# A four-layer graph network on one core: the second filter product is issued before the nodes' turn, and turns are inserted, removed and moved

## The chip, the core and the metric

The kernel runs on one NeuronCore of a Trainium2 chip. The number that counts is the device time of one execution, in microseconds. The kernel before takes 1591.17 us (median of three runs, 1591.0 to 1591.64). A profiled execution of it, from which all finer numbers here are read, took 1607.39 us, of which 1605.5 us lie between its first and its last instruction.

The engines are called as in the profile: PE (matrix products), PEld (its weight loads), DVE (vector work), ACT (activation functions), POOL (GpSimd), SP (issues DMAs).

## What is computed

128 graphs of 64 nodes, 128 features each, go through four layers. Every layer is `x = layernorm(x + f(x, adj))`. Cut to what matters:

```python
# layers 0 and 1: a continuous filter over the edges (i, j) with adj != 0
W   = ssp(gauss(adj) @ w1 + b1) @ w2 + b2          # filter of an edge: two products
agg[i] = sum_j  (x @ w_in)[j] * W[i, j] * c(adj[i, j])
out = ssp(agg @ o1 + c1) @ o2 + c2                 # "the nodes' turn"
# layer 2: graph convolution, norm_A from adj
h = elu(elu(x @ W0 + b0));  h = elu(norm_A @ (h @ W1) + b1)
out = norm_A @ (h @ W2) + b2
# layer 3
out = relu((A_norm @ x) @ W.T + b)
```

`ssp` is `softplus - log 2`. The entries of `adj` at 5.0 or more weigh nothing in layer 0, and zero entries carry one constant filter.

## The kernel before, in words

The function at work is `sparse_stack`. It treats the graphs in 64 pairs (`NP`), two graphs on the 128 partitions. The nodes of each graph are sorted so that the edges of a pair fill a compact list of slots. Preparing those lists (`gathering`, `compact`, `nearest`, `pack`) is vector work that is spread through the first half of the run as `early`, a few instructions per step.

**The main loop** is one Python loop over `i` that lays down the instruction streams, with `n, k = divmod(i, 3)`: `n` counts pairs (0 to 63 in layer 0, 64 to 127 in layer 1), and the slots of a pair are cut into three chunks `k`. A pass of the loop is called a step here. Each step works on three chunks at once, a pipeline of depth three: the current chunk `c`, the chunk before it `c1`, and the one before that, `c2`.

- `filter_in(c)`: first filter product (PE, tile `px`, line 1774), then the exponential (ACT).
- `gather(c1)`: product that fetches the features of the neighbours (PE, `pg`, line 1800), copied out by ACT.
- `softplus(c)`: the logarithm (ACT).
- `filter_out(c2)`: second filter product (PE, `pw`, line 1788).
- `message(c2)`: filter times features (DVE, `m`, line 1814). It empties `pw`.

`px`, `pg` and `pw` each have one PSUM buffer (`bufs=1`), of two banks. So the next `pw` may start only when `m` of the step before has read the last one, the next `px` only when the exponential has read the last, and the next `pg` only when its copy is done.

At `k == 0` a step also builds the weighted one-hot matrix for the gather (`hot`, DVE, line 1762), asks SP for the data of two pairs later, and starts preparing features for a later group (`ahead`). At `k < 2` ACT computes one half of the next pair's Gaussians (`d`). At the start of each step `run(sums, ...)` lays down some of the nine reductions of a pair's messages (`agg`, DVE, lines 1837 and 1841), and `run(early, ...)` some of the preparation.

**Turns.** The rest is written as Python generators, and a `yield` ends a turn. Each kind of work has a queue, and `slot(queue)` gives its first generator one turn. A turn that ends in `yield True` has just issued products into a bank of `ps_n` (two banks in all). The instruction that empties this bank is laid down not at once but inside the next call of `slot` for another queue, after that queue's own turn (the variable `owing`). The queues:

- `befores`: `node_before`, features for a group of four pairs: transposes `xT`, one turn; product `y`, one turn (lines 1444 and 1453). It also adds a bias on POOL (line 1449).
- `nodes`: `node_after`, once for each group of four pairs when its reductions are complete. In layer 0 first `zero_share` (transposes `zT`, product `zs`); then product `u` (line 1565), product `o` (1584), product `back` (1593), and a layer norm: two turns of statistics on DVE (lines 1415 and 1416), one turn on POOL (1422, 1423, and four of 1428, which write `x_all`).
- `convs[0]` and `convs[1]`: `graph_convs`, layers 2 and 3 for one group of four pairs, for even and odd groups. It starts when the group's layer 1 is done, and runs through the products `gx` (transposes), `gh`, `hw`, `nT` (transposes), `gh`, `hw`, `o`, a layer norm, `nT`, `sup`, `o`, and a layer norm. Its rows are stored by four scatters issued by POOL (`stores`, one per step).
- `last`: three queues for the last pairs (groups of two, one and one pairs), which run node work and convolutions in one chain.

A group of four pairs takes twelve steps. "Place 0" to "place 11" below mean the steps of a group, place 0 being `k = 0` of its first pair. In each step, PE's order before the change is `px`, `pg`, the nodes' turn, at `k == 1` the turn of `befores`, the turns of `last`, `pw`, then the turn of `convs[0]` and that of `convs[1]`. `in_order` pins the streams of all five engines to the order in which they are laid down, so no engine passes a waiting instruction.

After the loop, the tail gives one turn to each queue in rounds until all are empty:

```python
    run(sums, -1)
    while nodes or convs[0] or convs[1] or any(last.values()) or stores:
        for queue in (*last.values(), nodes, *convs):
            slot(queue)
        run(stores, 1)
```

Of the kernel before, what the change touches and what calls it, by code (L numbers as in the profile page):

```python
# [601 lines left out]
def sparse_stack(ctx: ExitStack, tc: tile.TileContext, t: dict, out: bass.AP, flag):  # L602
# [14 lines left out]
    NP = NB // 2  # L617
    GS = 4
# [12 lines left out]
    def pair_at(n):  # L631

        return n // NP, (n + 8 * (n // NP)) % NP
# [168 lines left out]
    def wait_steps(n):  # L802
        yield from (None for _ in range(n))
# [583 lines left out]
    def bank(name, n=GS):  # L1387
        ps = ps_n.tile([P, 512], F32, tag="n", name=name)[:, 0 : n * P]
        return ps, ps.rearrange("p (s c) -> p s c", s=n)
# [163 lines left out]
    def node_after(layer, q, agg):  # L1553


        w = layers[layer]
        name = f"{layer}_{q}"
        n = agg.shape[1]
        codes = node_codes.pop((layer, q))
        if layer == 0:  # L1560
            yield from zero_share(q, agg)
        elif q < len(GROUPS[1]) - 1:
            yield
        u, _ = bank(f"u_{name}", n)
        nc.tensor.matmul(
            u, lhsT=w["o1"], rhs=agg.rearrange("f s r -> f (s r)"), start=True, stop=True
        )
        yield True
        a, h = once("na", n, q), once("nh", n, q)
        act(h, u, AF.Identity, bias=w["c1"])  # L1570
        act(a, h, AF.Abs)
        act(a, a, AF.Exp, scale=-1.0)
        yield
        act(a, a, AF.Ln, scale=0.5, bias=half)

        back = once("bk", n, q)
        nc.vector.tensor_scalar(back, codes, row[:, 0:1], None, ALU.is_equal)
        back = by_pair(back)
        yield
        nc.vector.scalar_tensor_tensor(h, h, 0.0, a, ALU.max, ALU.add)  # L1580
        yield
        _, ps = bank(f"o_{name}", n)
        for s in range(n):
            nc.tensor.matmul(  # L1584
                ps[:, s, :], lhsT=h[:, s * P : (s + 1) * P], rhs=w["o2"], start=True, stop=True
            )
        yield True
        o = by_pair(once("no", n, q))
        act(o, ps, AF.Copy)
        yield  # L1590
        _, ps = bank(f"back_{name}", n)
        for s in range(n):
            nc.tensor.matmul(ps[:, s, :], lhsT=back[:, s, :], rhs=o[:, s, :], start=True, stop=True)
        yield True
        y = by_pair(once("ny", n, q))
        xs = x_all[:, GROUPS[layer][q], :]
        nc.vector.tensor_add(y, ps, xs)
        yield
        yield from layernorm(y, xs, n, name)
        if layer == 1:  # L1600
            if n < GS:
                yield from graph_convs(q)
            else:
                convs[q % 2].append(graph_convs(q))
# [58 lines left out]
    def graph_convs(q):  # L1663
# [3 lines left out]
        n = xs.shape[1]  # L1667
# [11 lines left out]

        if n == GS:  # L1680
            scaled(2, q)
            yield from wait_steps(2)
        flat, ps = bank(f"gx_{q}", n)
        for s in range(n):
            nc.tensor.transpose(ps[:, s, :], xs[:, s, :], ident)
# [36 lines left out]
        else:  # L1722
            nT3 = normals[3, q]
        y3 = yield from times("sup", lambda s: xs[:, s, :], lambda s: nT3[:, s, :])
        flat, ps = bank(f"o3_{q}", n)
        nc.tensor.matmul(
            flat, lhsT=ones, rhs=g["b3"][:, 0:n, :].rearrange("i s c -> i (s c)"),
# [147 lines left out]
    N = 2 * NP  # L1875
# [12 lines left out]

    def ahead(n):

        layer, p = pair_at(n + GS)
        for q, group in enumerate(GROUPS[layer]):
            if group.start == p:
                befores.append(node_before(layer, q))
# [21 lines left out]
    for i in range(3 * N + 2):  # L1916
# [1 line left out]
        c, c1, c2 = None, *past  # L1918


        run(sums, (1, 4, 4)[k])
        run(early, 9 if i < 18 else (PACE - 2, PACE + 1, PACE + 1)[k] if i < 3 * (NP - 8) else 7)
        run(side, min(2, len(side)))
        run(stores, 1)
# [13 lines left out]
        if n < N:  # L1938
            layer, p = pair_at(n)
            q = next(q for q, group in enumerate(GROUPS[layer]) if group.start <= p < group.stop)  # L1940
            c = dict(
                id=f"{n}_{k}", n=n, k=k, s=p - GROUPS[layer][q].start, at=(layer, q), w=layers[layer],
                size=CHUNKS[layer][p // 8],
            )
            if k == 0:
                if n + GS < N:
                    ahead(n)
                if n + 2 < N:
                    slot_data[n + 2], late = later_loads(n + 2)
                if c["s"] == min(2, len(range(NP)[GROUPS[layer][q]]) - 1):  # L1950
                    load_nodes(layer, q)
                if n > 0:
                    one_hot(n)
                if layer == 1 and c["s"] == 0 and q in last:
                    last[q].append(normals_of(q))
            if k == 1 and n + 2 < N:
                late()
            filter_in(c)
        if c1 is not None:
            gather(c1)  # L1960
        if c is not None:
            softplus(c)
            if k == 2 and sines:

                sines.popleft()()
        slot(nodes)
        if k == 1 and befores:
            slot(befores)
        for queue in last.values():
            slot(queue)  # L1970
        if c2 is not None:
            filter_out(c2)
            message(c2)
        if convs[0]:
            slot(convs[0])
# [59 lines left out]
```

## Time and profile before

| what | value |
|---|---|
| median of three runs | 1591.17 us |
| profiled execution / its span | 1607.39 us / 1605.5 us |
| PE busy | 1432.6 us, 89% |
| DVE busy | 1355.6 us, 84% |
| ACT busy | 1335.6 us, 83% |
| POOL busy | 732.5 us, 46% |
| main loop, first to last `px` | 75.3 to 1526.7 us |
| layer 0 in a group of twelve steps (`px` to `px`, 221 to 629 us) | 39.8 to 43.0 us |
| layer 1 in a group of twelve steps (878 to 1426 us) | 48.6 to 50.8 us |
| tail, from the last reductions of the loop | 1545.9 to 1605.5 us |

How to read it: busy time is summed over stages that differ. In layer 0 the preparation still runs and DVE is as busy as PE; in layer 1 the convolutions have joined and PE is the fullest; in the tail no engine is full. A wait counts only in the stage in which it lies. The time of a step is read from the starts of its `px`, and what ended an engine's idle time stands in brackets in the timeline.

### The profile page before, as it was taken

How to read it: one execution, taken by the hardware profiler on the slowest of the kernel's cores; microseconds unless marked ns; L12 is line 12 of the kernel's file. 1: busy time of each engine (PE TensorE's matmuls, PEld its weight loads, DVE VectorE, ACT ScalarE, POOL GpSimd, SP SyncE). 2: the span in 40 equal slices, each digit the busy share in tenths (PEclk: the TensorE clock that was granted, in tenths of full speed). 3: DMA queues.
4: the chain of work that ended last, by engine and by line, in shares of the span. 5: the costliest groups of instructions: out<-in, count | busy, mean ns of one | idle time of the engine just before them, and what ended most of it. 6: DMA issues, size and time to landing. Idle time of an engine off the chain costs nothing.

```text
span 1605.5 us, 24221 instructions
## 1 busy us (share of the span) xinstructions
PE 1432.6 (89%) x6813; PEld 802.6 (50%) x6813; DVE 1355.6 (84%) x3547; ACT 1335.6 (83%) x1847; POOL 732.5 (46%) x1174
## 2 busy tenths in 40 slices
PE   1276999999999999999999999999999999999974
PEld 1133454555554555555445555556555555555543
DVE  7687889999989999889878888888888888888873
ACT  1266898989888989889999998999989999899842
POOL 2425246555655644425611255433554435543454
PEclk9998999999999999999999999999999999999976
DMA  7654464645455544447555455544554455455200
GB/s 257 209 123 114 112 138 123 135 124 145 124 136 134 136 122 113 113 111 178 149 151 129 128 142 132 129 124 125 144 132 120 120 134 138 124 141 123 64 8 23
DMA packets 122289, 205.67 MB, mean 128 GB/s; under 512 B 47956, under 2 KB 80034, under 8 KB 121506
## 3 DMA queue, kind: packets, MB, share of 16 engines
q1 hardware_dynamic: 110784, 187.61, 46.7%
q0 software_dynamic: 6576, 14.99, 2.9%
q10 hardware_dynamic: 4786, 1.43, 0.4%
q8 instruction: 57, 0.93, 0.3%
q14 instruction: 86, 0.70, 0.2%
HBM read 185.29 MB, written 18.64 MB: 127 GB/s over the span
## 4 chain that ended last, share of the span: by engine, by line
PE 45%; DVE 27%; ACT 10%; DMA 7%; issue 6%; SPq 3%; POOL 2%; another core or an unknown queue 1%; ACTq 0%; DVEq 0%; POOLq 0%
PE pw L1788 16%; PE px L1774 9%; DVE m L1814 8%; PE pg L1800 7%; DVE agg L1837 6%; ACT h L951 4%; DVE hot L1762 2%; DVE at L1182 2%; PE hw L1673 2%; SPq L1299 2%; ACT g L951 2%; PE y L1453 2%; ACT d L951 1%; DVE st L1415 1%; PE o L1584 1%
## 5 line engine op out<-in xcount | busy, mean ns | idle before, releaser
L951 ACT ACTIVATE h<-h,half 128x672 f32<-128x672 f32 (+13 forms) x385 | 353.1, 917 | 0.1
L1837 DVE TENSOR_REDUCE agg<-m 128x16 f32<-128x240 f32 (+13 forms) x896 | 325.0, 411 | 3.0
L951 ACT ACTIVATE g<-pg 128x672 f32<-128x672 f32 (+12 forms) x384 | 303.2, 790 | 26.4 <-DVE m L1814 13.2
L1800 PE MATMUL pg<-hot,ys 64*128 64x336 f32 (+12 forms) x1536 | 308.8, 478 | 7.9 <-DVE hot L1762 7.0
L1788 PE MATMUL pw<-h,w_L_gnn_W2T 128*128 128x420 f32 (+5 forms) x768 | 301.9, 516 | 15.2 <-DVE m L1814 15.2
L1814 DVE SCALAR_TENSOR_TENSOR m<-pw,c_L_gnn_b,g 128x840 f32<-128x840 f32 (+5 forms) x192 | 200.9, 1046 | 115.6 <-PE pw L1788 88.0
L1788 PE MATMUL pw<-h,w_L_gnn_fw 128*128 128x336 f32 (+6 forms) x768 | 264.4, 467 | 28.3 <-DVE m L1814 22.0
L951 ACT ACTIVATE h<-px,c_L_gnn_b 128x840 f32<-128x840 f32 (+5 forms) x192 | 178.7, 931 | 53.6 <-PE px L1774 52.8
L1814 DVE SCALAR_TENSOR_TENSOR m<-pw,c_L_gnn_fb,g 128x672 f32<-128x672 f32 (+6 forms) x192 | 176.9, 921 | 50.0 <-PE pw L1788 31.2
L951 ACT ACTIVATE h<-px,c_L_gnn_fb 128x672 f32<-128x672 f32 (+6 forms) x192 | 159.3, 830 | 71.2 <-PE px L1774 46.4
L1788 PEld LDWEIGHTS pw<-h,w_L_gnn_W2T 128*128 128x128 f32 x768 | 132.5, 191 | 141.1 <-DVE m L1814 37.6
L1774 PE MATMUL px<-d,fw 64*128 64x336 f32 (+6 forms) x768 | 166.2, 507 | 40.8 <-DMA d<-d_dram 29.2
L1800 PEld LDWEIGHTS pg<-hot,ys 64*128 64x128 f32 x1536 | 146.3, 188 | 108.1 <-issue 17.5
L1788 PEld LDWEIGHTS pw<-h,w_L_gnn_fw 128*128 128x128 f32 x768 | 132.5, 191 | 120.6 <-DVE m L1814 62.2
L1762 DVE SCALAR_TENSOR_TENSOR hot<-j,row,w 128x1212 f32<-128x1212 bf16 (+12 forms) x128 | 177.0, 1383 | 9.0 <-issue 9.0
L1774 PE MATMUL px<-d,w1t 64*128 64x420 f32 (+5 forms) x768 | 181.1, 548 | 1.7 <-ACT h L951 1.6
L1422 POOL TENSOR_SCALAR rs<-mv 128x4 f32<-128x4 f32 x61 | 14.5, 237 | 344.0 <-DVE mv L1416 335.6
L1774 PEld LDWEIGHTS px<-d,fw 64*128 64x128 f32 x768 | 59.7, 188 | 132.2 <-ACT h L951 44.4
L951 ACT ACTIVATE d<-d,neg_off 128x1212 f32<-128x1212 f32 (+12 forms) x128 | 119.8, 936 | 7.1 <-issue 7.1
L1428 POOL TENSOR_SCALAR x_all<-ny,mv,rs 128x128 f32<-128x128 f32 x124 | 116.4, 947 | 3.3
L1030 POOL DMA_INDIRECT rows<-comb,goes x64 | 67.9, 1061 | 97.1 <-DMA rows<-comb,goes 69.6
L1774 PEld LDWEIGHTS px<-d,w1t 64*128 64x128 f32 x768 | 57.8, 184 | 66.8 <-ACT g L951 26.8
(264 smaller groups left out, 2209.6 us busy)
## 6 DMA issues: line engine op xcount, KB each, us to landing
d<-d_dram SPq DMA_DIRECT2D x32, 315.0 KB
w<-w_dram SPq DMA_DIRECT2D x32, 315.0 KB
d<-d_dram SPq DMA_DIRECT2D x32, 303.0 KB
w<-w_dram SPq DMA_DIRECT2D x32, 303.0 KB
w<-w_dram SPq DMA_DIRECT2D x32, 252.0 KB
j<-j_dram SPq DMA_DIRECT2D x32, 157.5 KB
j<-j_dram SPq DMA_DIRECT2D x32, 151.5 KB
d<-d_dram SPq DMA_DIRECT2D x16, 300.0 KB
```

The costliest lines, as they stand in the source:

```text
L951: latest = nc.scalar.activation(out_, in_, func, **kw)
L1030: nc.gpsimd.indirect_dma_start(out=into, out_offset=bass.IndirectOffsetOnAxis(ap=at, axis=0), in_=rows, in_offset=None,)
L1182: nc.vector.max_index(out=at[:, r, cut], in_max=top[:, r, cut], in_values=av[:, r, :])
L1299: (engine if name == "d" else nc.sync).dma_start(to, dram_ap(slots[layer, name][s], first, [[0, to.shape[0]], [1, n]]))
L1428: (nc.gpsimd if n == GS else nc.vector).tensor_scalar(dst[:, s, :], y[:, s, :], mv[:, s, 0:1], rstd[:, s : s + 1], ALU.subtract, ALU.mult,)
L1453: nc.tensor.matmul(ps[:, s, :], lhsT=xt[:, s * P : (s + 1) * P], rhs=w["win"], start=True, stop=True)
L1762: nc.vector.scalar_tensor_tensor(hots[n][:, 0:size], j[:, 0:size], near, wt[:, 0:size], ALU.is_equal, ALU.mult)
L1774: nc.tensor.matmul(ps[:, b, 0:n], lhsT=w1, rhs=d[rows, col : col + n], start=True, stop=True)
L1788: nc.tensor.matmul(c["pw"][:, b, :], lhsT=c["w"]["w2"], rhs=c["h"][:, b, :], start=True, stop=True)
L1800: nc.tensor.matmul(ps[:, b, 0:n], lhsT=y[rows, :], rhs=hots[c["n"]][rows, at], start=True, stop=True,)
L1814: nc.vector.scalar_tensor_tensor(messages[n][:, :, at], c["pw"], c["w"]["b2"], c["g"], ALU.add, ALU.mult)
L1837: nc.vector.tensor_reduce(av[:, :, :, r], both, AX.X, ALU.add)
```

## The change

The products and activations are the same, and in the same numbers. What changes is where they are laid down.

- In a step, `filter_out(c2)` moves from behind the nodes' turn to in front of it: PE's order becomes `px`, `pg`, `befores`, `pw`, `last`, nodes, `convs[0]`, `convs[1]`. `message(c2)` stays behind the nodes' turn. What empties a bank of the nodes is therefore laid down behind `message` (inside the turn of the convolutions), where before it was laid down in front of it.
- The turn of `befores` moves to just behind `gather`; it comes at `k == 2` in layer 0 and at `k == 0` in layer 1, where before it came at `k == 1`. `ahead` looks three pairs ahead, not four.
- `node_after` loses a turn of waiting in front of `u` in layer 1 (all groups but the last), and gains one in front of the layer norm in layer 0.
- `graph_convs` of full groups loses two turns of waiting in front of `gx`, and gains one between `sup` and the last product.
- The reductions are laid down as 1, 5, 4 in layer 0 (before: 1, 4, 4) and as 2, 4, 5 in layer 1, for `k` = 0, 1, 2. A pair has eight turns of reductions, the last of two instructions.

```diff
@@ -1559,8 +1559,6 @@
         if layer == 0:
             yield from zero_share(q, agg)
-        elif q < len(GROUPS[1]) - 1:
-            yield
         u, _ = bank(f"u_{name}", n)
@@ -1596,6 +1594,8 @@
         nc.vector.tensor_add(y, ps, xs)
         yield
+        if layer == 0:
+            yield
         yield from layernorm(y, xs, n, name)
@@ -1679,7 +1679,6 @@
         if n == GS:
             scaled(2, q)
-            yield from wait_steps(2)
         flat, ps = bank(f"gx_{q}", n)
@@ -1722,6 +1721,8 @@
         y3 = yield from times("sup", lambda s: xs[:, s, :], lambda s: nT3[:, s, :])
+        if n == GS:
+            yield
         flat, ps = bank(f"o3_{q}", n)
@@ -1888,7 +1889,7 @@
     def ahead(n):

-        layer, p = pair_at(n + GS)
+        layer, p = pair_at(n + 3)
@@ -1918,7 +1919,7 @@
-        run(sums, (1, 4, 4)[k])
+        run(sums, ((1, 5, 4), (2, 4, 5))[n >= NP][k])
@@ -1943,7 +1944,7 @@
             if k == 0:
-                if n + GS < N:
+                if n + 3 < N:
                     ahead(n)
@@ -1958,18 +1959,19 @@
         if c1 is not None:
             gather(c1)
+        if k == (0 if n >= NP else 2) and befores:
+            slot(befores)
         if c is not None:
             softplus(c)
...
-        slot(nodes)
-        if k == 1 and befores:
-            slot(befores)
+        if c2 is not None:
+            filter_out(c2)
         for queue in last.values():
             slot(queue)
+        slot(nodes)
         if c2 is not None:
-            filter_out(c2)
             message(c2)
         if convs[0]:
             slot(convs[0])
```

## The prediction

> **What bounds the kernel now.** First the windows: PE, DVE, ACT and POOL busy by stage.
>
> ```profile
> 400.00:600.00 200.00, 186.76 (x914) 102.90 (x913) 189.55 (x603) 172.83 (x261) 109.53 (x178) 1.00 0.53 132
> ...
> 1200.00:1400.00 200.00, 194.00 (x963) 113.65 (x963) 167.92 (x363) 183.42 (x237) 95.70 (x117) 1.00 0.51 129
> ...
> 1550.00:1606.00 56.00, 29.50 (x143) 23.10 (x142) 23.57 (x84) 16.50 (x51) 25.12 (x33) 0.71 0.06 18
> ```
>
> The columns are the stretch, its length, then busy time (and count) of PE, PEld, DVE, ACT and POOL, the granted clock, DMA share and GB/s. In layer 0 (first line) PE with 186.76 and DVE with 189.55 of 200 are both full; in layer 1 PE is (194.00); in the tail nobody. So an order can win only what PE idles. The waits from 880 to 1425 us, eleven groups of layer 1 with all convolutions, say for what (us, times, longest):
>
> ```profile
> DVE m L1814 <- PE pw L1788: 61.2, 49, 2.7
> ACT h L951 <- PE px L1774: 41.9, 65, 1.2
> ...
> PE pw L1788 <- DVE m L1814: 14.1, 22, 1.1
> ```
>
> PE's only wait of size is `pw` for `m`, 22 times: twice a group. The windows put PE at 529.3 of these 545 us, 15.7 idle. PE's timeline shows where they lie:
>
> ```profile
> 1222.69 0.93 PE L1774 MATMUL px<-d,w1t 64*128 64x392 f32 x4
> 1223.45 0.82 PE L1800 MATMUL pg<-hot,ys 64*128 64x392 f32 x4
> 1224.21 1.58 PE L1788 MATMUL pw<-h,w_L_gnn_W2T 128*128 128x392 f32 x4
> 1225.72 0.93 PE L1774 MATMUL px<-d,w1t 64*128 64x392 f32 x4
> 1226.49 0.82 PE L1800 MATMUL pg<-hot,ys 64*128 64x392 f32 x4
> 1228.34 1.58 PE L1788 MATMUL pw<-h,w_L_gnn_W2T 128*128 128x392 f32 x4 [1.03 <-DVE m L1814]
> 1229.86 0.92 PE L1774 MATMUL px<-d,w1t 64*128 64x384 f32 x4
> 1230.60 0.82 PE L1800 MATMUL pg<-hot,ys 64*128 64x392 f32 x4
> 1231.70 1.58 PE L1788 MATMUL pw<-h,w_L_gnn_W2T 128*128 128x392 f32 x4 [0.27 <-DVE m L1814]
> ```
>
> These are places 10, 11 and 0. The starts of `px` in this group give steps of 4.2, 4.3, 3.0, 3.5, 4.8, 4.3, 3.9, 5.0, 4.4, 4.8, 3.0 and 4.1 us for places 0 to 11. A step with no small product lasts 3.02 (`px` to `px` above, places 10 to 11: 1.52 to `pw`, 1.5 on); place 11 has none and lasts 4.1, since DVE is late with `m`:
>
> ```profile
> 1222.24 1.02 DVE L1814 SCALAR_TENSOR_TENSOR m<-pw,c_L_gnn_b,g 128x784 f32<-128x784 f32 x1
> ...
> 1227.27 1.02 DVE L1814 SCALAR_TENSOR_TENSOR m<-pw,c_L_gnn_b,g 128x784 f32<-128x784 f32 x1
> ...
> 1230.63 1.01 DVE L1814 SCALAR_TENSOR_TENSOR m<-pw,c_L_gnn_b,g 128x784 f32<-128x784 f32 x1
> ```
>
> Between the first two lie 5.03 us of DVE work without a gap (two pairs of statistics, an elu, four reductions), while PE has 3.97 between its `pw`. The stall is one of balance: three places (2, 10, 11) carry no small product, place 7 three.
>
> **What the Trainium skill says.** "PSUM — Partial Sum Buffer", section "Engine vs sequencer instructions": the queues of ScalarE, VectorE and GpSimdE are strictly first-in-first-out, and matmuls start in program order. The trace agrees: the `px` behind the late `pw` came at 1229.86, 4.14 after the one before. "Perfetto Trace Analysis", "Optimization Strategy": consistent bubbles, the same gap repeated, can mean too few buffers. So here: one `pw` buffer, the gap of 1.0 us every twelve steps; the change leaves the buffer and moves what surrounds it. Same page, "Identifying the Most-Contended Engine": matmul busy time is no measure of closeness to the roofline. So I use distances between starts, not 97% busy.
>
> **Part by part, layer 1.** Moving `pw` in front of the nodes only turns the ring: between two `pw` PE still does `px`, `pg`, nodes, two convolutions, and DVE still owes one `m`. That alone costs or saves nothing. What counts is which place each product and each DVE piece lands in. Distances from the DVE timeline (start to start): `m` 0.95, `hot` 1.36, a reduction 0.35 (the last two 0.6), two pairs of statistics 0.81, elu 1.3, other pieces 0.6, `bk` 0.4. PE: transposes 0.45, other products 0.9 to 1.05, the last with its bias 1.3.
>
> Counting turns in the new code, the node chain starts one step sooner (`u` at place 4), convolutions start at place 0 with `gx` at once (before: places 1 and 3), `xT` falls in place 3, `y` in 6. Below, L is PE's distance from `pw` of the place to the next `pw` without waits, W the DVE work from this `m` to the next.
>
> | place | 0 | 1 | 2 | 3 | 4 | 5 | 6 | 7 | 8 | 9 | 10 | 11 |
> |---|---|---|---|---|---|---|---|---|---|---|---|---|
> | L before | 4.4 | 4.0 | 3.0 | 4.4 | 4.8 | 3.5 | 4.0 | 6.3 | 4.5 | 4.0 | 3.0 | 3.0 |
> | W before | 2.2 | 3.0 | 3.5 | 3.0 | 3.7 | 3.6 | 3.4 | 3.0 | 4.7 | 5.1 | 3.2 | 3.2 |
> | L after | 3.5 | 3.9 | 3.9 | 4.0 | 4.9 | 5.7 | 4.0 | 4.0 | 4.0 | 4.0 | 4.0 | 3.0 |
> | W after | 2.4 | 4.0 | 3.6 | 2.2 | 3.1 | 4.8 | 3.7 | 3.5 | 5.0 | 2.4 | 3.3 | 3.8 |
>
> DVE's lag grows by W − L where positive and shrinks where negative; PE waits where the lag exceeds L − 2.7 (1.65 from `pw` to `m`, 0.95, 0.1). Before: the lag is 0.2 after place 8, 1.3 after 9; at place 10 L − 2.7 is 0.3, a wait of 1.0, and 0.1 at place 11. The trace has 1.03 and 0.27, so the sum describes it. After: lag 0.8 out of place 11, just L − 2.7 at place 0, gone by 1; 1.0 out of place 8, against 1.3 at place 9. No wait. So 1.3 us a group go. Eleven full groups: −14. Groups 18, 30 and 31 have the same wait in part, and in group 30 a third product in a step waits 1.5 us for its bank (`xt`), which with at most two per step falls away: −3.
>
> What hides the rest. ACT: its pieces in place 4 rise to 5.7 us (`u`'s three, `hw`'s copy, Gaussians) against PE 4.9, followed by 3.0 against 5.7; before, places 5 and 6 stood 1.7 over PE and no `px` waited over 0.4. POOL: the two removed turns stood between POOL's writing of `x_all` and `gx`. POOL needs 0.23, 1.04 and 3.87 plus gaps for it, 5.3 in all (the norm at 1230.82 to 1236.15). Counted from `pw` of place 7, the statistics end in place 10 at 13.0, POOL comes free behind two scatters and a scaling (1.1, 1.1 and 2.6 with its wait) at 13.2, `x_all` is ready at 18.5, and PE, at the end of `pw` of place 0, asks for it at 20.5. Cost nothing, with 2.0 us of cover; below, what if it is gone. Behind `gx` in PE's queue stand the other convolution and the next `px`, so a wait there is a wait of the whole loop. `sup` has 2.2 us of cover behind POOL's next norm. The turn of `befores` takes its ACT copies and its POOL addition (1.3) with it; its features are due only two pairs later. The SP queue is untouched, and scatters keep one per step.
>
> **Layer 0.** 1, 5, 4 lays down what 1, 4, 4 did, since a pair has no more. `xT` and `y` go from places 1 and 4 to 5 and 8; the statistics from 0 and 1 to 1 and 2. With the preparation at 0.4 us in a `k = 0` step and 1.0 in the others (an estimate from DVE's fullness), the same sum gives 2.5 us of waits a group before (in the trace: groups of 40.1, less the 37.6 that PE needs, twelve bare steps of 2.65 and 5.8 of node products) and 2.9 after: places 1 to 4 lose their cover, just where statistics now fall. Twelve groups: +5. Against it, no node product stands between `pg` and `pw` any more, so `pg`'s waits for `hot` (4.5 us from 200 to 600) hurt less: −2. Unknown from both sides: −15 (half of all layer-0 waits go) to +12 (preparation 0.3 heavier at the bad places).
>
> **Tail.** Its rounds follow the chain of the last pair; the last full group runs beside it. At the end:
>
> ```profile
> 1593.59 3.12 POOL L1428 TENSOR_SCALAR gz<-gz,mv,rs 128x128 f32<-128x128 f32 x4
> 1596.74 0.18 DVE L1416 BATCH_NORM_AGGREGATE mv<-st 128x2 f32<-128x6 f32 x1 [3.20 <-POOL gz L1428]
> ```
>
> DVE waits 3.2 us for a statistics buffer that POOL still reads. The full group now runs two rounds sooner (nodes one, `gx` two, less one), so its norm no longer meets this; a wait of about 1 may remain two rounds earlier. −3, bounds 0 and −7.
>
> **Sum.** −14 −3 +3 −3 = −17, on 1607.39: 1590. The same on the median of 1591.17: **1574 us**.
>
> **Rivals.**
> 1. Larger gain: the pipeline before suffers in layer 0 from products between `pg` and `pw`, and many of its waits go too. For it: ten waits of `pw` and `pg` there, up to 1.3. Against: DVE is at 95%, its work stays. A third of the waits, 12 × 2.5 / 3 = 10, goes instead of +3: −14 −3 −10 −3 = −30, so 1562.
> 2. The gap moves: DVE's lag of 0.8 and 1.0 stands so close to L − 2.7 that 0.3 more per step brings waits back (0.3 a group by the same sum), and layer 0 takes its +12: 1591 − 17 + 4 + 9 = 1587.
> 3. Slower: POOL. If `x_all` comes 4.2 us later than I count, `gx` stalls PE by 2.2 in each of twelve groups, +26: 1600. It decides from 3.4 late on (2.0 of cover, 17/12 to eat up the gain). For it: POOL waits up to 2.1 for its own scatters ahead of other work (14.1 us in ten waits before `blocks`), and two can stand ahead. Against: in the sum they are there once.
>
> **Chances.** Forecast 0.52 (own range 1566 to 1582), larger gain 0.14, moved gap 0.18, POOL 0.16. A difference of 0.2% (3.2 us) is about what can be told from none; of rival 2, 0.07 lie within. Faster 0.77, same 0.07, slower 0.16. Range 1560 to 1595: below it a third of rival 1, above it most of rival 3.
>
> **What would show it.** Right: `pw`'s waits for `m` in layer 1 under 5 us (14.1), `px` to `px` at place 11 about 3.0, groups near 48.2 us for 49.5; layer-0 groups within 1 us of before; no 3.2 us wait at the end. Wrong: waits of `gx` for `x_all`, of `px` for ACT, groups of layer 0 above 42, or `pw` waiting at places 0 and 9.

## The result, and the profile after

The kernel after takes 1599.8 us (median of 20 runs, 1589.64 to 1615.04) against 1591.69 us for the kernel before (20 runs, 1590.1 to 1597.96). The ratio is 1.0036, 95% interval 1.0022 to 1.005: it is slower by 0.2 to 0.5%, where 1574 us was forecast. The longest run of after, 1615.04 at a granted clock of 0.976 (the others: 0.979 to 0.985), counts as slow and is left out of the ratio. The runs of before lie within 8 us, the other 19 of after within 18.

The profiled execution of after took 1594.84 us, with a span of 1593.0. That it is shorter than the profiled one of before (1607.39) is no contradiction. That one lies outside the 20 timed runs: it has one step of 15.0 us in group 1 (place 6, from `px` to `px`), the same step of after takes 4.5, and groups 0 and 1 together take 103.5 against 89.2 us. The stall is found in single executions of kernels with and without the change (more on it below). Without these two groups, the two profiles compare as follows; the columns are sums of `px`-to-`px` steps in us, and `stores_k12_b` is a kernel of the experiments below. The sum is +0.9 (of unrounded steps) where the medians differ by 8.1, since after's profiled execution is a short one (1594.84) and before's has 2.8 us in group 8 (43.0 for 40.2) that `before_no_stores` has not; a second trace of after gives +4.6.

| part of the run | forecast | before | after | difference | `stores_k12_b` | difference to before |
|---|---|---|---|---|---|---|
| groups 2 to 13, layer 0 | +3 | 490.5 | 497.4 | +6.9 | 499.0 | +8.5 |
| groups 14 to 18 | in the -3 below | 209.2 | 211.8 | +2.6 | 211.7 | +2.5 |
| groups 19 to 29, layer 1 | -14 | 547.3 | 542.0 | -5.3 | 533.6 | -13.7 |
| group 30 to the last `px` | -3, with group 18 | 100.9 | 102.2 | +1.3 | 96.9 | -4.0 |
| last `px` to the end | -3 | 78.8 | 74.3 | -4.5 | 74.4 | -4.4 |
| sum | -17 | | | +0.9 | | -11.1 |

First the windows of after, for the same stretches of the main loop as before; the columns are the stretch, its length, busy time and count of PE, PEld, DVE, ACT, POOL, then clock, DMA share and GB/s.

```profile
400.00:600.00 200.00, 185.69 (x908) 105.23 (x908) 191.21 (x606) 173.73 (x261) 109.39 (x176) 1.00 0.53 130
1200.00:1400.00 200.00, 194.94 (x965) 115.64 (x964) 167.82 (x363) 182.17 (x235) 102.48 (x112) 1.00 0.50 129
```

PE's busy time in layer 1 hardly moves (194.00 before, 194.94). POOL's is the one that grows: 95.70 before, 102.48 now, with the same work in hand. Busy shares thus hide both the gain and the loss; the waits from 880 to 1420 us show them.

```profile
DVE m L1815 <- PE pw L1789: 69.5, 77, 3.8
POOL blocks L1630 <- DMA out_dram<-gz,at_row: 34.6, 19, 2.8
ACT h L951 <- PE px L1775: 24.3, 52, 0.8
...
PE sup L1673 <- POOL x_all L1428: 6.2, 17, 0.5
...
PE gx L1684 <- POOL x_all L1428: 1.3, 1, 1.3
```

The wait that the change was costed for, `pw` for `m` (14.1 us before), isn't in this list any more as a wait of PE, and the wait of ACT's `h` for `px` fell from 41.9 to 24.3. In its place stands a wait that before has not: PE's `sup` for POOL's `x_all`. And POOL itself waits 34.6 us for its own scatters in front of `blocks` (the scalings of the adjacency, line 1630), where before it was 14.1 (the prediction quoted that number in its third rival). Before had another wait of this kind, though, in front of the next scatter, which the prediction left out and after has no more:

```profile
POOL out_dram L1030 <- DMA out_dram<-gz,at_row: 15.7, 10, 1.6
```

So in sum they were 29.8 and are 34.6: what changed is above all where they lie. The page of after has for the whole run, in its rows of groups (line, engine, operation, count, then busy time, mean ns of one, idle before):

```profile
L1789 PE MATMUL pw<-h,w_L_gnn_W2T 128*128 128x420 f32 (+5 forms) x768 | 306.1, 521 | 1.2 <-DVE m L1815 1.2
L1789 PE MATMUL pw<-h,w_L_gnn_fw 128*128 128x336 f32 (+6 forms) x768 | 271.8, 477 | 33.1 <-DVE m L1815 33.0
...
L1030 POOL DMA_INDIRECT out_dram<-gz,at_row x56 | 78.1, 1395 | 14.1 <-POOL blocks L1630 4.5
```

The first row is layer 1, the second layer 0, the third are the scatters of finished rows. In before the same rows are:

```profile
L1788 PE MATMUL pw<-h,w_L_gnn_W2T 128*128 128x420 f32 (+5 forms) x768 | 301.9, 516 | 15.2 <-DVE m L1814 15.2
L1788 PE MATMUL pw<-h,w_L_gnn_fw 128*128 128x336 f32 (+6 forms) x768 | 264.4, 467 | 28.3 <-DVE m L1814 22.0
L1030 POOL DMA_INDIRECT out_dram<-gz,at_row x56 | 59.7, 1066 | 30.0 <-DMA out_dram<-gz,at_row 20.8 <-POOL blocks L1630 4.5 <-issue 2.4
```

In layer 1 the wait for `m` went from 15.2 to 1.2 us, in layer 0 it grew from 22.0 to 33.0, and a scatter takes 1395 ns for 1066, though it moves the same rows.

Where does the new wait lie? The step at place 3, where `sup` now stands, takes 4.4, 5.5, 5.5, 4.4, 4.4, 4.3, 6.4, 5.5, 5.4, 6.3, 6.3, 6.4 and 7.3 us in groups 19 to 31. Below, the length without a wait is seen to be 4.2 to 4.4. Place 11 now takes 3.0 to 3.1, as forecast (4.1 before). PE's timeline at place 3 of group 25:

```profile
1182.18 1.48 PE L1789 MATMUL pw<-h,w_L_gnn_W2T 128*128 128x392 f32 x4
1183.50 0.39 PE L1673 MATMUL sup<-nTs,x_all 128*128 128x128 f32 x2
1184.39 0.49 PE L1673 MATMUL sup<-nTs,x_all 128*128 128x128 f32 x2 [0.50 <-POOL x_all L1428]
1185.16 0.49 PE L1673 MATMUL sup<-nTs,x_all 128*128 128x128 f32 x2 [0.29 <-POOL x_all L1428]
1186.13 0.49 PE L1673 MATMUL sup<-nTs,x_all 128*128 128x128 f32 x2 [0.48 <-POOL x_all L1428]
1186.55 0.93 PE L1775 MATMUL px<-d,w1t 64*128 64x392 f32 x4
```

`sup` runs piece by piece at the pace at which POOL writes the four pieces of `x_all`: it lasts 3.1 us from its start to the next `px`, where without a wait it takes 1.0. Waits of this kind are split between the records of PE and PEld, and so the list of waits understates them; the step says it whole.

Why is POOL late? Its timeline for the groups 25 and 24, with DVE's `hot` (the one-hot matrix, built once a pair) in between. Group 25 first:

```profile
1168.89 3.14 POOL L1428 TENSOR_SCALAR x_all<-ny,mv,rs 128x128 f32<-128x128 f32 x4
1171.89 1.44 DVE L1763 SCALAR_TENSOR_TENSOR hot<-j,row,w 128x1176 f32<-128x1176 bf16 x1
1172.21 2.08 POOL L1030 DMA_INDIRECT out_dram<-gz,at_row  x1 [0.18 <-issue]
1174.34 0.62 POOL L1630 TENSOR_TENSOR blocks<-a_all,dinv 64x256 f32<-64x256 f32 x1
1177.01 0.61 POOL L1630 TENSOR_TENSOR blocks<-a_all,dinv 64x256 f32<-64x256 f32 x1 [2.05 <-DMA out_dram<-gz,at_row]
1177.70 1.27 POOL L1688 TENSOR_TENSOR x_all<-x_all,b_L_gnn_b 128x512 f32<-128x512 f32 x1
...
1181.68 4.40 POOL L1428 TENSOR_SCALAR x_all<-gz,mv,rs 128x128 f32<-128x128 f32 x4
1182.23 1.43 DVE L1763 SCALAR_TENSOR_TENSOR hot<-j,row,w 128x1176 f32<-128x1176 bf16 x1
```

The same stretch one group before, where place 3 took 4.4:

```profile
1120.49 3.14 POOL L1428 TENSOR_SCALAR x_all<-ny,mv,rs 128x128 f32<-128x128 f32 x4
1123.78 1.44 DVE L1763 SCALAR_TENSOR_TENSOR hot<-j,row,w 128x1176 f32<-128x1176 bf16 x1
1123.81 1.10 POOL L1030 DMA_INDIRECT out_dram<-gz,at_row  x1 [0.18 <-issue]
1124.94 0.75 POOL L1630 TENSOR_TENSOR blocks<-a_all,dinv 64x256 f32<-64x256 f32 x1
1126.32 0.61 POOL L1630 TENSOR_TENSOR blocks<-a_all,dinv 64x256 f32<-64x256 f32 x1 [0.62 <-PE pg L1801]
1127.01 1.28 POOL L1688 TENSOR_TENSOR x_all<-x_all,b_L_gnn_b 128x512 f32<-128x512 f32 x1
...
1130.98 3.14 POOL L1428 TENSOR_SCALAR x_all<-gz,mv,rs 128x128 f32<-128x128 f32 x4
1134.22 1.43 DVE L1763 SCALAR_TENSOR_TENSOR hot<-j,row,w 128x1176 f32<-128x1176 bf16 x1
```

Read the two side by side, from the end of the first norm. In group 25 the third scatter begins 0.32 us after `hot`, lasts 2.08, and the second scaling behind it waits 2.05 for the transfer to land. In group 24 the scatter and `hot` begin within 0.03 us of each other, the scatter lasts 1.10, and the scaling waits 0.62. So the next norm begins 9.65 us after the end of the norm before in one case, 7.35 in the other. That is not all: being late, the norm of group 25 has the next `hot` inside it, and takes 4.40; in group 24 it ends 0.1 before `hot`, and takes 3.14. `x_all` is ready 1.3 us before `sup` asks for it (1134.12, asked for at 1135.44) or 2.6 after (1186.08, 1183.50).

This isn't a matter of two groups. Of the 48 scatters between 820 and 1500 us, the 25 that had no `hot` beside them lasted 1.02 us on average, none over 1.10. In 20 others `hot` began 0.10 to 0.56 us sooner than the scatter; each of these ended 0.97 to 1.00 us after `hot` had ended, and so lasted 1.82 to 2.40. It is as if the scatter began only then. The last three began within 0.05 us of `hot` and lasted 1.10; they are those of groups 22 to 24, whose steps at place 3 are the only ones of 4.3 and 4.4 but for group 19. The same holds in the three traces with this order in layer 1 (after, and `after_again` and `layer0_back` below), groups 20 to 31, 36 cases: in 24 the third scatter is lengthened and place 3 takes 5.4 us or more; in 9 it lasts 1.10 and place 3 takes 4.2 to 4.4. The three left over are group 28 in each trace: its scatter lasts 1.10 with no `hot` beside it, but the norm in front of it has `hot` inside, the scaling behind it still waits 2.65 to 3.41 us for the landing, and place 3 takes 6.3 to 7.0.

Why the landing takes so much longer after a late scatter is not shown. What the traces show is other traffic: SP issues the next pair's loads of `j` and `w` from 1125.25 us on in group 24, after the scatter's end (1124.91), but from 1173.36 on in group 25, before it (1174.29). In the 3 us after the scatter's end the busy share of the DMA engines is 0.49 in group 24, 0.82 in group 25 and 1.00 in group 28. No run moves these loads.

In before, `hot` overlaps ten scatters by more than 0.05 us; eight of them began first and lasted 1.0, one met `hot`'s last 0.4 us and took 1.24, and one took 2.15. With norms of four it is the same: 3.14 us alone, 3.89 to 4.75 with a whole `hot` inside. The Trainium skill has the mechanism, "SBUF — State Buffer", section "🔬 SBUF: two separate sides": VectorE and GpSimd share a pair of ports, which is an exclusive lock and no sharing of bandwidth; a VectorE instruction with two inputs in SBUF takes it against GpSimd work that reads SBUF, whichever starts first has it for its whole instruction, and a DMA issued by GpSimd is kept from writing its descriptors while VectorE runs an instruction in a two-port mode. `hot` reads two tiles of SBUF (`j` and `w`), and a scatter reads its row numbers (`at_row`) from SBUF; that a two-input instruction holds up a DMA the section does not say, and here it is measured. The trace agrees where `hot` is first, down to the end at a fixed distance behind it. Where the scatter is first the page would have `hot` wait, and there the traces show both at work at once: in before, eight times for 0.11 to 0.92 us, with `hot` at its 1.4 to 1.5 us. Which ports are used no trace can show.

The end of the tail was forecast to lose most of a wait of 3.20 us of DVE for a buffer that POOL still reads. In after:

```profile
1581.45 3.14 POOL L1428 TENSOR_SCALAR gz<-gz,mv,rs 128x128 f32<-128x128 f32 x4
1584.62 0.18 DVE L1416 BATCH_NORM_AGGREGATE mv<-st 128x2 f32<-128x6 f32 x1 [1.86 <-POOL gz L1428]
```

1.86 of it is left, and the tail as a whole is shorter by 4.5.

### The profile page after: what moved, and what is told of

Same layout as the page of the kernel before. It is cut to its first block, busy times and chain, and to the rows that moved or that the text cites. A ratio compares the mean times of both kernels' runs of the same rounds, so it can differ in the third digit from the quotient of the medians.

```text
span 1593.0 us, 24199 instructions
## 1 busy us (share of the span) xinstructions
PE 1433.9 (90%) x6813; PEld 819.3 (51%) x6813; DVE 1359.8 (85%) x3547; ACT 1339.7 (84%) x1847; POOL 768.2 (48%) x1174
## 3 DMA queue, kind: packets, MB, share of 16 engines
q10 hardware_dynamic: 4786, 1.43, 0.4%
## 4 chain that ended last, share of the span: by engine, by line
PE 41%; DVE 16%; POOL 14%; DMA 12%; ACT 6%; issue 6%; SPq 5%; POOLq 0%; DVEq 0%; ACTq 0%
PE pw L1789 15%; PE px L1775 9%; PE pg L1801 7%; DMA out_dram<-gz,at_row 5%; POOL x_all L1428 5%; DVE m L1815 4%; SPq L1299 3%; ACT h L951 3%; DVE agg L1838 2%; POOL gz L1428 2%; POOL rs L1423 2%; DMA w<-w_dram 2%; DVE at L1182 1%; PE y L1453 1%; PE hw L1673 1%
## 5 line engine op out<-in xcount | busy, mean ns | idle before, releaser
L1838 DVE TENSOR_REDUCE agg<-m 128x16 f32<-128x240 f32 (+13 forms) x896 | 319.6, 411 | 2.9
L1789 PE MATMUL pw<-h,w_L_gnn_W2T 128*128 128x420 f32 (+5 forms) x768 | 306.1, 521 | 1.2 <-DVE m L1815 1.2
L1789 PE MATMUL pw<-h,w_L_gnn_fw 128*128 128x336 f32 (+6 forms) x768 | 271.8, 477 | 33.1 <-DVE m L1815 33.0
L1422 POOL TENSOR_SCALAR rs<-mv 128x4 f32<-128x4 f32 x61 | 17.3, 284 | 385.5 <-DVE mv L1416 383.6
L1428 POOL TENSOR_SCALAR x_all<-ny,mv,rs 128x128 f32<-128x128 f32 x124 | 106.7, 868 | 3.3
L1030 POOL DMA_INDIRECT out_dram<-gz,at_row x56 | 78.1, 1395 | 14.1 <-POOL blocks L1630 4.5
```

Of the source, the lines that this page charges most:

```text
L1030: nc.gpsimd.indirect_dma_start(out=into, out_offset=bass.IndirectOffsetOnAxis(ap=at, axis=0), in_=rows, in_offset=None,)
L1422: nc.gpsimd.tensor_scalar(rstd, mv[:, :, 1], LN_EPS, None, ALU.add)
L1428: (nc.gpsimd if n == GS else nc.vector).tensor_scalar(dst[:, s, :], y[:, s, :], mv[:, s, 0:1], rstd[:, s : s + 1], ALU.subtract, ALU.mult,)
L1789: nc.tensor.matmul(c["pw"][:, b, :], lhsT=c["w"]["w2"], rhs=c["h"][:, b, :], start=True, stop=True)
L1838: nc.vector.tensor_reduce(av[:, :, :, r], both, AX.X, ALU.add)
```

## The experiments

Two chips show the kernel before at different times (1592 and 1607 us), so each is compared with before on its own chip. The expectations call the theories by short names: POOL, that PE's new wait comes from POOL's late `x_all`; POOL-BY-STORES, that it is the scatters that make POOL late; LOCK, that it is those beside `hot`; RING, that moving `pw` alone only turns the order of a step round. Steps at place 3 and sums over groups are from the `px` of each trace.

### The kernel after once more

> The changed kernel once more, with a trace of another execution. Theory POOL: in layer 1 `sup` (place 3) waits for POOL's `x_all`, which stands behind the store scatters, and the length of a scatter differs from execution to execution. So about 1599 us, a wide spread (1590 to 1608), and in the trace the steps at place 3 of groups 19 to 31 between 4.4 and 7.5 us and different from those of the first trace, all other steps of layer 1 equal to it within 0.1 us. Rival LAYER 0: the loss is in layer 0, which is then over 8 us longer than before (groups 2 to 13: 491 us before, 497 after in the first trace), with place 3 of layer 1 under 4.6.

1599.93 us (1589.85 to 1611.87, 22 runs); ratio 1.0046 (1.0027 to 1.0065). Place 3 of groups 19 to 31: 4.4, 4.4, 6.5, 7.2, 4.4, 5.5, 6.4, 5.5, 6.3, 7.0, 6.3, 5.5, 4.2, so the long ones are in other groups than in the first trace, and groups 19 to 29 take 550.9 us for 542.0. The wait is decided anew in every group and execution, as a race would be, and the time spreads with it.

All other steps were expected to stay within 0.1 us, and two do not: place 4 takes 6.4 and 6.3 us in groups 25 and 29, for 4.8 and 4.7. There the granted clock falls just after the wait of `sup`. Group 25, with a line of the windows (length, busy time of PE, clock, DMA share, GB/s):

```profile
1188.53 0.49 PE L1673 MATMUL sup<-nTs,x_all 128*128 128x128 f32 x2 [0.64 <-POOL x_all L1428]
1188.95 1.52 PE L1775 MATMUL px<-d,w1t 64*128 64x392 f32 x4
1190.25 1.52 PE L1801 MATMUL pg<-hot,ys 64*128 64x392 f32 x4
1190.00:1192.00 2.00, 2.00 (x7) 0.50 0.81 174
```

The clock is 0.50 for 3.4 us, and `px` and `pg` take 1.52 us each where they took 0.93 and 0.82. So a late `x_all` can cost 1.6 us more than its wait. It happens in two of the nine late groups here, in none in the first trace; what decides it stays open.

### `sup` a turn later

```diff
-        y3 = yield from times("sup", ...)
         if n == GS:
             yield
+        y3 = yield from times("sup", ...)
```

> The turn that the change adds behind `sup` is put in front of it, so that `sup` is asked for one step (some 3.5 us) later. Theory POOL: the waits at place 3 (12 us in the first trace, some 17 in a median run) go: 1582 us, 1578 to 1588, and the spread shrinks to under 6 us. Rival LAYER 0 (or the order of the step itself): no more than 4 us gained, 1596 to 1600, spread as wide as before.

1584.58 us (1581.83 to 1587.91); ratio 0.9948 (0.9932 to 0.9965). Place 3 takes 3.3 to 3.5 in all groups; `sup` now falls in place 4, which takes 5.9 to 6.1 for 4.7 to 4.9. Groups 19 to 29: 534.7. POOL is as late as in after (a scatter of 2.09, a wait of 1.73, a norm of 4.71 in group 25), only nobody waits for it. This shows that the late partner is POOL's `x_all`, and that 7 to 16 us hang on it in groups 19 to 29, the difference to the two traces of after.

### The scatters of full groups left out

The 56 scatters of the full groups aren't made, so those rows of the output aren't written.

```diff
-            stores.append(store_rows(pairs, z))
+            if n < GS:
+                stores.append(store_rows(pairs, z))
```

> The rows of the full groups in pairs 8 to 63 are not stored: 56 scatters fewer on POOL, all else as in the changed kernel. Theory POOL-BY-STORES: POOL has some 8 us per group more and `x_all` is in time for `sup`; the waits of PE at place 3 are 0, 1580 us, 1575 to 1586, spread under 4 us. Rival POOL-BY-ITS-OWN-WORK: the norms, the scalings and the bias addition (about 19 us a group) are already late without stores; place 3 still waits over 0.5 us in most groups, 1592 or more.

> The kernel before, with the 56 scatters of the full groups left out (their rows are not written), as in no_stores for the kernel after. There that was worth 26 us. POOL-BY-STORES: before, only few scatters lie beside hot and POOL is late for nobody, so here they are worth little: -1 to -6 us against before, steps of layer 1 unchanged at 3.4 to 3.7 at place 3. If scatters cost their time in any order (traffic, POOL's share), it is -15 to -26 here too.

In the kernel after: 1573.41 us (1572.58 to 1577.14), ratio 0.9881 (0.9861 to 0.9902), 26 us under after and more than expected; place 3 takes 4.2 to 4.4 in every group, and groups 19 to 29 take 530.1. Of the 26 us, 12 to 21 lie there and some 4 to 5 in the tail (69.5 for 74.3 and 73.6). In the kernel before: 1590.25 us against 1592.78, ratio 0.9981 (0.997 to 0.9992), 2.5 us, and groups 19 to 29 take 547.3 in its trace, as with them. So the scatters themselves are nearly free where POOL has room. They are dear only in the order of the kernel after, and with them go the wait and the spread.

### No scatter in the step that builds `hot`

`hot` is built at `k == 0`.

```diff
-        run(stores, 1)
+        if k:
+            run(stores, 1)
```

> The changed kernel, with no store scatter laid down in k = 0 steps (they come one per step at k = 1 and 2), so the third scatter of a group no longer stands in POOL's queue just where DVE builds the one-hot matrix (`hot`), and only one more stands in front of the norm that `sup` waits for. Theory LOCK: a scatter is as long as its 1.0 us plus the time for which `hot` runs beside it (1.86 to 2.3 us against 1.01 in the traces), and POOL's lateness is made of these; the waits of `sup` go: 1582 us, 1578 to 1588, spread under 8 us. Rival COUNT: it is the number of POOL instructions, which is the same; 1595 or more, spread as wide as before.

> The same kernel as stores_k12, for comparison with best_b on one chip. The group sums give -20 to -27 us in layer 1 and its neighbour stages against after with late POOL: -5 to -9 us against before where before has no stall in group 1 (median near 1592), -20 where it has (median near 1607).

1586.47 us (1585.44 to 1590.2) where before took 1607.13, ratio 0.9872 (0.9838 to 0.9907); on another chip 1583.19 (1577.56 to 1589.29) where before took 1592.78, ratio 0.9924 (0.9902 to 0.9947). Of the 20.7 us on the first chip only a part is the edit's: the other traces from it have the stall of group 1 (102.6 to 104.1 us in groups 0 and 1), this one has less of it (94.5). Place 3 takes 4.2 to 4.4 everywhere, groups 19 to 29 take 533.4 and 533.6. POOL's timeline of `stores_k12`, for the stretch of group 25 shown of after:

```profile
1174.37 3.14 POOL L1428 TENSOR_SCALAR x_all<-ny,mv,rs 128x128 f32<-128x128 f32 x4
1177.49 2.37 POOL L1630 TENSOR_TENSOR blocks<-a_all,dinv 64x256 f32<-64x256 f32 x2
1179.94 1.29 POOL L1688 TENSOR_TENSOR x_all<-x_all,b_L_gnn_b 128x512 f32<-128x512 f32 x1
1181.40 1.11 POOL L1030 DMA_INDIRECT out_dram<-gz,at_row  x1 [0.18 <-issue]
...
1184.05 3.14 POOL L1428 TENSOR_SCALAR x_all<-gz,mv,rs 128x128 f32<-128x128 f32 x4
...
1188.88 1.05 PE L1673 MATMUL sup<-nTs,x_all 128*128 128x128 f32 x8
```

`hot` still costs POOL something: the two scalings take 2.37 beside it, where they took 0.6 each elsewhere. But no transfer is waited for, the next norm begins 6.5 us after the one before has ended (9.65), stays clear of `hot`, and ends at 1187.19, 1.7 before `sup`. No work was taken away, just one POOL instruction was moved by a step; what the forecast saw for layer 1 is there (-13.7 for -14). The edit also leaves one scatter fewer between the two norms, but that alone is not it: group 24 above has the scatter there, not lengthened, and its norm is in time. Of the 3.1 us between 9.65 and 6.5, 2.3 separate groups 25 and 24. Nor are all scatters clear of `hot` now: the first of each group still begins behind it and lasts 1.85 to 2.15 in `stores_k12_b`, where nobody is late for it. The third scatter's start beside `hot`, and the landing that is waited for behind it, are the cause of the new wait, but for group 28, where `hot` falls into the norm in front.

### Layer 0's turns as before

```diff
-        if layer == 0:
-            yield
...
-        layer, p = pair_at(n + 3)
+        layer, p = pair_at(n + (3 if n >= NP - 3 else GS))
...
-                if n + 3 < N:
+                if n + 3 < N and n != NP - 4:
...
-        if k == (0 if n >= NP else 2) and befores:
+        if k == (0 if n >= NP else 1 if n < NP - 3 else 2) and befores:
```

> The turns of layer 0 as before the change: features at k = 1 (still in front of the second filter product) and asked for four pairs ahead, no added turn in front of its layer norm. Layer 1 as changed. Theory COVER: layer 0's groups 2 to 13 lose the 7 us that they gained (497 to 490 to 492); the total falls by 5 to 8 us against the changed kernel, about 1593, the wide spread stays. Rival ORDER: the order of the step costs that time, not the turns; no change, 1598 to 1601.

1596.05 us (1585.84 to 1607.23); ratio 1.0014 (0.9994 to 1.0035). That is 3.9 under after, less than expected, and the total can't tell it from before, as layer 1's race is still in it. The groups can: groups 2 to 13 take 489.8, for 497.4 and 495.3 in the two traces of after and 490.5 before. So layer 0's part of the change costs 5.5 to 7.6 us in these traces. Part of it is the clock again: group 3 in the first trace takes 4.5 us at place 4 (2.8 in the second), in a stretch of 3.4 us with a granted clock of 0.50.

### The two together, and with `sup` later too

> Both repairs together: stores at k = 1 and 2 only, and layer 0's turns as before the change. If the two losses are separate they add: 6 us less than the kernel with the stores moved alone, about 1576 us, 1572 to 1581. Rival: layer 0's loss is made good elsewhere (in the wait of its last groups for data); no more than 2 us less, 1580 to 1584.

> The same kernel as best. ADD: layer 0's 7 us come on top of stores_k12_b wherever before has no stall in group 1: 5 to 10 us below stores_k12_b. START: the old turns of layer 0 give the stall of group 1 back on this chip too (step of over 10 us at place 6): within 3 us of stores_k12_b.

> As the one with both repairs, and the added turn in front of `sup` too. Theory: with the stores moved nothing is late for `sup`, so its later place only makes place 4 fuller (6.0 us against 4.8) and place 3 emptier: 0 to +3 us against it. Rival: some lateness of POOL is left; 3 to 6 us less.

`best` has both of the last two edits. On the chip with before at 1607 it took 1587.77 (1586.61 to 1589.21), no gain on `stores_k12` beside it: its trace has a step of 15.4 us in group 1, and 102.6 us in groups 0 and 1 for 94.5. On the other chip the same kernel took 1572.4 (1570.36 to 1581.29), 10.8 under `stores_k12_b` beside it and 20.4 under before, ratio 0.9874 (0.985 to 0.9898), with 89.7 us for groups 0 and 1 and 488.6 for groups 2 to 13. There the gains of both layers do add. This version beats before by about 20 us on either chip (after was not run on the first). The chain that ended last, first in after, then in `best_b`, each from its page:

```profile
PE 41%; DVE 16%; POOL 14%; DMA 12%; ACT 6%; issue 6%; SPq 5%; POOLq 0%; DVEq 0%; ACTq 0%
```

```profile
PE 59%; DVE 21%; DMA 6%; issue 4%; ACT 3%; SPq 3%; POOL 3%; ACTq 0%; DVEq 0%; POOLq 0%
```

POOL and DMA, 26% of the way to the end in after, are 9% in `best_b`, as they are in before. The edit of `sup_later` on top makes it worse, and by more than the 0 to 3 us expected: 1598.59 (1592.88 to 1605.62), 10.8 over `best` on the same chip. In the traces groups 19 to 29 take 2.7 us more and the steps from group 30 on 5.2, with one of 8.3 at place 4 of group 31. That POOL being in time leaves nothing to hide fits the theory; why it costs this much wasn't followed further.

### `pw` moved alone, and the turns alone

`order_only` is the kernel before with `filter_out(c2)` in front of `slot(nodes)`; `turns_only` is the kernel after with it moved back (its edit is shown).

```diff
-        if c2 is not None:
-            filter_out(c2)
+        slot(nodes)
         for queue in last.values():
             slot(queue)
-        slot(nodes)
         if c2 is not None:
+            filter_out(c2)
             message(c2)
```

> The kernel before, with the second filter product moved in front of the nodes' turn and nothing else changed (the features' turn keeps its place at k = 1, in front of the second filter product). Theory RING, as in the prediction: moving it only turns the ring of products; within 3 us of before, 1589 to 1595. Rival: the order itself wins time, since DVE gets the second filter product sooner in a step with node products: 5 us or more less. Or it costs time in layer 0, where the node products no longer stand between `pg` and `pw`: 5 us or more more.

> The kernel after with pw moved back behind the nodes' turn; all turns as after. TURNS: the turns alone make both the gain in layer 1 (pw's wait for m at place 11 gone) and the new wait of sup, so this takes after's time: +0 to +12 us against before with a wide spread, place 3 at 4.4 to 7. ORDER: if the second product's place carries part of the gain, pw waits for m again and it is 8 us or more over after: +13 to +22 against before.

`order_only`: 1607.27 us beside before's 1607.13, ratio 1.0000 (0.9984 to 1.0015). Groups 19 to 29 take 543.0 for 547.3 (place 11 3.6 for 4.1), group 30 to the last `px` 104.3 for 100.9. Alone, the move is worth nothing in sum, as forecast. It is not without effect, though: PE's wait of `pw` for `m` from 880 to 1425 us falls from 14.1 to 8.1.

`turns_only`: 1626.19 us (1625.34 to 1634.46), ratio 1.0217 (1.0191 to 1.0242): 33 us over before and some 26 over after. Both expectations named less, and TURNS falls. But ORDER's mechanism isn't it either: `pw` waits for `m` just 3.1 us from 880 to 1425, and place 11 takes 3.0. What is new are steps of 5.7 to 6.5 us at place 0 in groups 25 to 29 (3.4 to 3.5 in after but for one of 4.9), in addition to those at place 3; in three of them (25, 27, 29) the granted clock is 0.50 after the wait, as above. Its timeline just ahead of group 25:

```profile
1164.18 4.98 POOL L1428 TENSOR_SCALAR gz<-gz,mv,rs 128x128 f32<-128x128 f32 x4
...
1167.06 1.44 DVE L1763 SCALAR_TENSOR_TENSOR hot<-j,row,w 128x1176 f32<-128x1176 bf16 x1
...
1174.28 0.61 POOL L1630 TENSOR_TENSOR blocks<-a_all,dinv 64x256 f32<-64x256 f32 x1 [3.19 <-DMA out_dram<-gz,at_row]
...
1177.74 4.22 POOL L1428 TENSOR_SCALAR x_all<-ny,mv,rs 128x128 f32<-128x128 f32 x4
...
1180.46 0.33 PE L1684 MATMUL gx<-ident,x_all 128*128 128x128 f32 x1 [1.52 <-POOL x_all L1428]
```

Here `hot` falls into POOL's norms, which last 4.98 and 4.22, and 20 of its 38 norms of four from 820 to 1500 us have a whole `hot` inside (9 of 39 in after, 1 of 39 in `stores_k12_b`). It is 13 of 38 in before too, but there nobody comes near to waiting: `x_all` is ready 8 us before `gx` begins. POOL is then late for `gx` also, which is rival 3 of the prediction at the place it named. So the move of `pw` is worth nothing before and some 26 us with the new turns: it seems to decide beside which of POOL's instructions `hot` comes to lie. That is read from the trace, and no further change tries it.

## Why the prediction was wrong

**The step that failed** is the removed turns of the convolutions, which were costed at nothing: "Cost nothing, with 2.0 us of cover", and "`sup` has 2.2 us of cover behind POOL's next norm". The cover is the time from the end of POOL's norm to the start of the product that needs it. In before it is 8.0 to 8.6 us for `gx` and 3.8 to 5.7 for `sup` (1.2 in group 31). In after, groups 20 to 31, it is 0.0 to 0.8 for `gx` (0.2 in group 25: the norm ended at 1172.03, `gx` began at 1172.26; and -1.7 in group 28, the one wait of `gx` in the list), and for `sup` 1.3 to 1.5 in three groups and -1.6 to -2.6 in nine. So the two turns before `gx` held time that POOL needed for scatters, scalings and norms; that it was they, and not the other moved turns, is read from these distances, as no run puts them back. The terms that were mis-sized: scatters at 1.1 us, where those behind `hot` took 1.82 to 2.40; a scaling "2.6 with its wait" counted once, where behind the third scatter another wait of 2.05 comes; and norms at 3.87, which take up to 4.75. All were taken as fixed durations from a trace in which most scatters lay beside nothing. The norm did not: the 3.87 has `hot` inside (1232.49 to 1233.93), against 3.14 alone, and the prediction did not ask what lengthened it. With the third scatter out of the way the cover of `sup` is 1.7 in group 25 (`stores_k12`; 1.5 to 2.6 in `stores_k12_b`), not far from the 2.2 counted. The price: groups 19 to 29 take 8.4 and 17.3 us more in the two traces of after than in `stores_k12_b`.

**Layer 1's balance was right.** The wait of `pw` for `m` went, place 11 fell to 3.0, and the sum of -14 is -13.7 where POOL is in time. In after, -5.3 and (second trace) +3.6 came of it.

**Layer 0 had the right sign and mechanism, and about half the size.** +3 was counted (+5 for lost cover, -2 for `pg`), +6.9 and +4.8 came; undoing it gave 5.5 to 7.6 back, and 10.8 in the total of `best_b`. The lost cover was the term too small: from 200 to 600 us PE's wait of `pw` for `m` grew from 11.1 to 19.5 (18.6 in the second trace), while `pg`'s wait for `hot` fell from 4.5 to 2.9 (3.1), about as counted. The forecast's "within 1 us" a group is met on average (0.6 and 0.4), not by each group (group 3 +2.4).

**The remainder.** The tail gave -4.5 for -3. The -3 of groups 18, 30 and 31 did not come in after (+1.3 from group 30 on), again for POOL: in `stores_k12_b` it is -4.0. Groups 14 to 18 cost 2.6, which no term of the sum held. Of these, 1.8 are group 18, in each trace with the new turns (47.5 for 45.7): PE has 217 products there for 201, so work has moved into it from later groups, which the -3 left out. The rest is mostly one step of group 15 (5.9 for 4.4); its cause stays open.

**The rivals.** The third had the engine right and was given 0.16. It put the stall at `gx` at every group alike, with a price of 26; it came at `sup`, in some of the groups, at about 8 to 17, and with layer 0's extra 2 to 4, the missing gain from group 30 on and the 2.6 of groups 14 to 18 that was enough to eat up the 17. Its argument against itself, "in the sum they are there once", was the error: on the way to `sup` POOL waits twice for its scatters (1.91 and 2.05 us in group 25).

## What to carry to other kernels

A turn of waiting that looks idle on the engine that bounds may be the slack of another one: before it is taken out, add up that engine's whole queue between its inputs and its deadline, with every wait for its own transfers. Durations on GpSimd hold only for what lay beside them on VectorE; after a reordering, ask which of its instructions now meets a long VectorE instruction with two operands in SBUF, and count its length on top, as with `hot` here. A wider spread of times after a reordering can point to a race decided anew each time; here the spread of 18 to 22 us was 5 and 12 (of five and six runs) with one scatter moved by a step, and 6 with `sup` a turn later.

## What was unexpected of the hardware

- A scatter issued on GpSimd lasted 1.02 us alone and up to 2.40 with `hot` (1.43 us) beside it, when `hot` began at least 0.1 us sooner; begun within 0.05 us of it or before it, 1.0 to 1.11. A norm of four pieces took 3.14 alone and up to 4.98 with `hot` and another instruction of this kind inside (`turns_only`).
- Lateness fed on itself: the scatter's delay of 1 us became 2.3 at the next norm's start, and by its longer duration 3.6 at the norm's end (group 25 against group 24, from the end of the norm before).
- A wait of PE was in some groups followed by 3.4 us at a granted clock of 0.50, with `px` at 1.52 us for 0.93 (`after_again`, group 25); in others, with waits as long, it was not.
- In some executions PE, DVE and ACT stand still in group 1, up to 15.4 us in one step, with no releaser that the profile shows, and then run on at a granted clock of 0.50 (149.8 to 163.4 us in `best`). Two of PE's waits in `best`'s trace; ACT waits 11.42 us beside them:

```profile
151.08 2.77 PE L1787 MATMUL pw<-h,w_L_gnn_fw 128*128 128x360 f32 x4 [4.58 <-issue]
158.42 2.07 PE L1534 MATMUL zs<-zt,ys 128*128 128x128 f32 x8 [4.57 <-issue]
```

All four traces from the chip on which before takes 1607 us have such steps in group 1 (of 8.3 to 15.4 us), none of the eight from the other chip has; the same kernel there takes 4.5 us at that place (`best_b`). What it is remains open; without taking it out, the two profiles of before and after would show a gain of 12.5 us where there is a loss of 8.1.
